# A recurrent layer gated by a feed-forward block: down projection of the gate in its own batch's stage, activation loads as ordinary steps, first gate and up weights fetched in the attention stage

## The chip, the cores and the metric

The kernel runs on one core of a Trainium2 chip. The metric is the time of one execution on the device in microseconds; the table below has three runs and one further execution, which was profiled. In the profile PE is TensorE (PEld its weight loads), DVE is VectorE, ACT is ScalarE, POOL is GpSimd, and SP is SyncE, whose queue issues nearly all DMAs here.

## The reference

Eight batches of 512 tokens with 512 features, all in float32. What is computed for each batch:

```python
xn = layernorm(x)
# recurrent part s
x_ssm, z = split(xn @ W_in.T)                    # 1024 + 1024 features
x_conv   = silu(causal_conv4(x_ssm) + conv_b)
p        = x_conv @ W_x.T                        # 16 B, 16 C, 1 step size
dt       = softplus(p[..., -1] + mean(dt_bias))
h_t      = exp(A * dt_t) * h_(t-1) + dt_t * B_t * x_t    # 1024 x 16 states
y_t      = sum_n(h_t * C_t)
s        = ((y + D * x_conv) * silu(z)) @ out_W.T
# gate g
attn = causal attention of rmsnorm(xn), 16 heads of 32; only attn @ A (rank 16) is used
mod  = 0.1 * tanh(attn @ A)
h    = rmsnorm(xn) * ln2_w
gate = silu(h @ W_in_base.T + mod * (h @ A) @ B)
up   = h @ W_up_base.T                           # 2048 features
g    = silu(xn + (gate * up) @ W_down.T)
out  = x + s * g
```

## The kernel before

The work has two stages. The first, the attention stage, runs over all eight batches: layer norm, attention down to the rank-16 modulation, and the transposed activations. It leaves for each batch `scr_x[b]` in DRAM (normalised x in its first half, the weighted `h` in the second) and the modulation in `scr_m[b]`. At its end it also does the convolutions and step sizes of batch 0 (`convolution(d)`, `steps_of_time`), and fetches xn and h of batch 0. Its tile pools are then given back, and the pools of the second stage (`wst`, `mp`, `scan`, `tmp`) are opened in their place; `wp` and `act` live through both.

The second stage is the scan. Each batch has 64 steps. A step k scans two channels of each of 32 groups for 16 states at once: a 128 x 1024 tile `x`, loaded from `scr_c` by broadcast (`load_scan`, issued four steps ahead into a ring of ten tiles), multiplied by dt*B (`inputs`, L487 on VectorE for even k, L489 on GpSimd for odd k, two steps ahead), scanned (`scan_step`, L495, VectorE, the decays written by ScalarE just before into a single `decay` buffer, L475), multiplied by C (`outputs`, L502, GpSimd). Every four steps the sum over states is a burst of small matmuls on TensorE (`sum_states`, L514), two steps after the last of the four; two bursts complete one block of 128 channels, and `finish_y` gates it with z on VectorE. The ring of `x` is released by these bursts.

Around the scan the dense work of TensorE is dealt out as a list of parts, `batch_parts(b)`. A part is a triple: its weight in units (a unit is one 128 x 128 by 128 x 512 float32 matmul), the loads it needs, and a function that issues its instructions and returns later pieces, each with a delay in chunks. A step has two chunks; in each chunk parts are issued until their units catch up with the share of the batch that has passed. The order on every engine is thus written out by the program, and each engine executes its own queue in that order. The parts of batch b, before:

- for b > 0, four times `finish(b-1, m)`: the down projection of the batch before (four parts of 4 units, L326; then `residual`, an add on VectorE and a tanh on ScalarE), the out projection (4 + 5 units, L342), then `product` (two VectorE operations, the first completes silu, the second multiplies by the out projection, L352 and L353), `turn` (four transposes), `add` (residual x) and `store`. The residual x is loaded as `fx` in `product`. The tiles are `f` and `xt`, two buffers each
- behind m = 1 an item `("h", load_h(b))`, and behind the four an item `("xn", load_xn(b+1))`
- eight pairs `gate_up` (17 units each, L275 and L284), with the convolutions of the next batch (`conv_in`, 4 units, L187) between them, and near the end `step_size(b+1)` (four projections of 2 units, then `turn`, which stores `scr_p` and reads it back three times as the broadcast B, C and dt)
- between them, eight z gates (`z_gate`, 4 units, L187, tanh L261, VectorE L255), at shares 0, 8/64, 16/64 and so on of the batch

For batches 1 to 6 this makes 136 + 32 + 64 + 36 + 9 + 32 = 309 units in 128 chunks. After the last batch the four `finish(7, m)` follow alone.

Loads go through `prefetch()`, called before and behind each part: it walks up to eight parts ahead and issues their loads in order, at most `limits[kind] - 1` outstanding of a kind, and stops at the first that it may not issue. An item of kind "xn" or "h" is issued only when it is itself the next part to run:

```python
if kind == "xn" or kind == "h":
    if state["load"] > state["run"]:
        return
```

The parts of a batch are put in the queue when its first step begins; those of batch 0 after the pools of the second stage are opened. `wgu` (gate and up weights, 512 KB, three buffers) is in the pool `wst`.

Of the kernel before, what the change touches and what calls it, by code (L numbers as in the profile page):

```python
# [10 lines left out]
F32 = mybir.dt.float32  # L11
AF = mybir.ActivationFunctionType
ALU = mybir.AluOpType
# [4 lines left out]
P = 128  # L18
NB = 8
S = 512  # L20
DM = 512
KT = DM // P
TT = S // P
DI = 1024
ND = DI // P
# [4 lines left out]
NF = 2048 // P  # L30
# [9 lines left out]
def mamba_gated_ffn_kernel(  # L40
# [22 lines left out]
    nc = tc.nc  # L63
# [18 lines left out]
    wp = ctx.enter_context(tc.tile_pool(name="w", bufs=1))  # L82
# [19 lines left out]
    def load_xn(b):  # L102
        xnt[b] = act.tile([P, KT, S], F32, tag="xnt", name=f"xnt_{b}")
        nc.sync.dma_start(xnt[b], scr_x[b][:, :KT, :])

    def load_h(b):
        ht[b] = act.tile([P, KT, S], F32, tag="ht", name=f"ht_{b}", bufs=1)
        nc.sync.dma_start(ht[b], scr_x[b][:, KT:, :])
        modh[b] = act.tile([2 * QD, S], F32, tag="modh", name=f"modh_{b}", bufs=1)
        for i in range(2):  # L110
            nc.sync.dma_start(modh[b][i * QD : i * QD + R, :], scr_m[b])
# [88 lines left out]
        loaded["win", b, c] = w  # L200

    def load_gu(b, f):
        w = wst.tile([P, 2, KT, P], F32, tag="wgu", name=f"wgu_{b}_{f}", bufs=3)
        nc.sync.dma_start(w, w_ffn[f][:, :2])
        loaded["wgu", b, f] = w

    def load_down(b, m, q):
        w = wst.tile([P, NF // 4, P], F32, tag="wd", name=f"wd_{b}_{m}_{q}", bufs=4)
        nc.sync.dma_start(w, w_ffn[ts(q, NF // 4), :, 2, m, :].rearrange("f p c -> p f c"))
        loaded["wd", b, m, q] = w  # L210
# [38 lines left out]
    def z_gate(b, d):  # L249

        st = {}

        def gate():
            t = tmp.tile([P, S], F32, tag="z", name=f"z_{b}_{d}")
            nc.vector.scalar_tensor_tensor(t, st["th"], 1.0, st["ps"], ALU.add, ALU.mult)  # L255
            gates[b, d] = t

        def run():
            ps = in_proj(b, ND + d)
            th = tmp.tile([P, S], F32, tag="th", name=f"zth_{b}_{d}", bufs=3)  # L260
            nc.scalar.activation(th, ps, AF.Tanh, scale=0.5)  # L261
            st.update(ps=ps, th=th)
            return [(1, gate)]

        return [(4, [("win", lambda: load_win(b, ND + d))], run)]
# [47 lines left out]
            (4, [], lambda: second(1)),  # L313
        ]

    def finish(b, m):

        st = {}

        def down(q):  # L320
            if q == 0:
                st["acc"] = bank(f"ps_acc_{b}_{m}")
            w = loaded.pop(("wd", b, m, q))
            for j in range(NF // 4):
                f = q * (NF // 4) + j
                nc.tensor.matmul(  # L326
                    st["acc"], lhsT=w[:, j, :], rhs=mlp[b, f], start=(f == 0), stop=(f == NF - 1)
                )
            return [(1, residual)] if q == 3 else []

        def residual():
            f = tmp.tile([P, S], F32, tag="f", name=f"f_{b}_{m}")
            nc.vector.tensor_tensor(f, st["acc"], xnt[b][:, m, :], ALU.add)
            nc.scalar.activation(st["acc"], f, AF.Tanh, scale=0.5)
            st["f"] = f

        def out_proj(q):
            if q == 0:
                st["ps"] = bank(f"ps_out_{b}_{m}")
            w = loaded["wout", b, m]  # L340
            for d in range(4 * q, 4 * q + 4):
                nc.tensor.matmul(  # L342
                    st["ps"], lhsT=w[:, d, :], rhs=xc[b, d], start=(d == 0), stop=(d == ND - 1)
                )
            if q == 1:
                loaded.pop(("wout", b, m))
                return [(1, product), (3, turn), (5, add), (7, store)]
            return []

        def product():  # L350
            f = st["f"]
            nc.vector.scalar_tensor_tensor(f, st["acc"], 1.0, f, ALU.add, ALU.mult)  # L352
            nc.vector.scalar_tensor_tensor(f, f, 0.5, st["ps"], ALU.mult, ALU.mult)  # L353
            xt = tmp.tile([P, TT, P], F32, tag="xt", name=f"fx_{b}_{m}")
            nc.sync.dma_start(xt, x[b, :, ts(m, P)].rearrange("(t p) c -> p t c", p=P))
            st["xt"] = xt

        def turn():
            ps = bank(f"ps_turn_{b}_{m}")
            for tt in range(TT):  # L360
                nc.tensor.transpose(ps[:, ts(tt, P)], st["f"][:, ts(tt, P)], ident)
            st["pt"] = ps

        def add():
            xt = st["xt"]
            nc.vector.tensor_tensor(
                xt, st["pt"].rearrange("p (t c) -> p t c", t=TT), xt, ALU.add
            )

        def store():  # L370
            nc.sync.dma_start(out[b, :, ts(m, P)].rearrange("(t p) c -> p t c", p=P), st["xt"])

        return [
            (4, [("wd", lambda q=q: load_down(b, m, q))], lambda q=q: down(q)) for q in range(4)
        ] + [
            (4, [("wout", lambda: load_out(b, m))], lambda: out_proj(0)),
            (5, [], lambda: out_proj(1)),
        ]
# [69 lines left out]
    STEPS = ND * 8  # L448
# [79 lines left out]

    def batch_parts(b):

        first = []
        if b > 0:
            for m in range(KT):
                first += finish(b - 1, m)
                if m == 1:
                    first.append((0, [("h", lambda: load_h(b))], lambda: []))
        pairs = [gate_up(b, fp) for fp in range(NF // 2)]
        convs, sizes = [], ([], [])
        if b + 1 < NB:
            convs = [conv_in(b + 1, d) for d in range(ND)]  # L540
            sizes = step_size(b + 1)
        rest = list(pairs[0])
        if b + 1 < NB:
            rest.insert(0, (0, [("xn", lambda: load_xn(b + 1))], lambda: []))
        for i in range(1, NF // 2):
            for _ in range(2 if i in (2, 4, 5) else 1):
                if convs:
                    rest += convs.pop(0)
            rest += pairs[i]
            if b + 1 < NB and i == NF // 2 - 3:  # L550
                rest += sizes[0]
            if b + 1 < NB and i == NF // 2 - 2:
                rest += sizes[1]
        parts = first + rest
        total = sum(p[0] for p in parts) + 4 * ND
        done, out_, z = 0, [], 0
        for p in parts:
            while z < ND and done >= total * (8 * z) / STEPS:
                out_ += z_gate(b, z)
                done += 4  # L560
                z += 1
            out_.append(p)
            done += p[0]
        while z < ND:
            out_ += z_gate(b, z)
            z += 1
        return out_

    queue = []
    limits = {"win": 3, "wgu": 3, "wd": 4, "wout": 2, "xn": 1, "h": 1}  # L570
    held = {}
    state = {"load": 0, "run": 0, "chunk": 0}
    later = {}

    def prefetch():
        while state["load"] < min(len(queue), state["run"] + 8):
            for kind, fn in queue[state["load"]][1]:
                if kind == "xn" or kind == "h":
                    if state["load"] > state["run"]:
                        return  # L580
                elif sum(held.values()) >= 0 and held.get(kind, 0) >= limits[kind] - 1:
                    return
                held[kind] = held.get(kind, 0) + 1
                fn()
            state["load"] += 1
# [22 lines left out]
    with ExitStack() as c1:  # L608
# [46 lines left out]
        for i in range(2):  # L655
            z = wa.tile([P, TT, HG, 4, 2 * R], F32, tag=f"z{i}", name=f"z{i}")
# [290 lines left out]
        sizes = step_size(0)  # L947

        def convolution(d):

            pair = ps_s.tile([P, 2, 512], F32, tag="s", name=f"s_conv_{d}")
            banks["special"] = lambda name: pair[:, 0, :]
            for delay, f in piece(conv_in(0, d)[0][2]):
                after(delay, f)
            banks["special"] = None
            if d + 3 < ND:
                load_win(0, d + 3)
            elif d == ND - 3:
                load_h(0)

        def steps_of_time(i):
            if i == 0:
# [83 lines left out]
    wst = ctx.enter_context(tc.tile_pool(name="wst", bufs=2))  # L1046
    mp = ctx.enter_context(tc.tile_pool(name="mp", bufs=NF))
    scan = ctx.enter_context(tc.tile_pool(name="scan", bufs=10))
    tmp = ctx.enter_context(tc.tile_pool(name="tmp", bufs=2))
# [6 lines left out]

    dtb_ps = ps_a.tile([P, S], F32, tag="dtb_ps", name="dtb_ps")

    queue.extend(batch_parts(0))
    for k in range(4):  # L1060
        load_scan(k)
        if k == 1:
            prefetch()
    inputs(0)
    inputs(1)
    decays(0)
# [1 line left out]
    for b in range(NB):  # L1068
# [3 lines left out]
        total = sum(p[0] for p in queue[n0:])  # L1072
        done = 0
        for s in range(STEPS):
            k = b * STEPS + s
# [15 lines left out]
    while bursts:  # L1091
        k = min(bursts)
# [72 lines left out]
```

## Time and profile before

| what | value |
|---|---|
| time, median of 3 runs | 3465.83 us (3461.27 to 3469.89) |
| profiled execution: its own time | 3461.55 us |
| profiled execution: span from first to last instruction | 3459.8 us, mean granted TensorE clock 0.973 |
| first scan / last scan begins | 884.80 us / 3361.76 us |
| VectorE scans, L495 | 512, mean 2285 ns |
| down projection, L326 | 1024 rows, 451.6 us busy |
| out projection, L342 | 512 rows, 226.9 us busy |
| gate and up, L275 | 2048 rows, 939.9 us busy |
| x loads for the scan | 512 of 512 KB |
| `wgu` / `win` / `wd` / `wout` loads | 128 of 512 KB / 128 of 256 KB / 128 of 256 KB / 32 of 512 KB |
| DMA over the span | 511.61 MB, 148 GB/s |

Each float32 matmul with 512 columns stands as two rows of about 0.43 us each, so a down projection of one m (16 matmuls) is 32 rows. The ends of matmuls are modelled and busy times of TensorE are unions of overlapping rows. A wait is put down to the engine or DMA that released it last.

### The profile page before, as it was taken

How to read it: one execution, taken by the hardware profiler on the slowest of the kernel's cores; microseconds unless marked ns; L12 is line 12 of the kernel's file. 1: busy time of each engine (PE TensorE's matmuls, PEld its weight loads, DVE VectorE, ACT ScalarE, POOL GpSimd, SP SyncE). 2: the span in 40 equal slices, each digit the busy share in tenths (PEclk: the TensorE clock that was granted, in tenths of full speed). 3: DMA queues.
4: the chain of work that ended last, by engine and by line, in shares of the span. 5: the costliest groups of instructions: out<-in, count | busy, mean ns of one | idle time of the engine just before them, and what ended most of it. 6: DMA issues, size and time to landing. Idle time of an engine off the chain costs nothing.

```text
span 3459.8 us, 33779 instructions
## 1 busy us (share of the span) xinstructions
PE 3224.3 (93%) x12058; PEld 1440.5 (42%) x12058; DVE 2539.9 (73%) x2782; ACT 1364.8 (39%) x2295; POOL 1898.1 (55%) x860
## 2 busy tenths in 40 slices
PE   7888888888788899999999999999999999999999
PEld 4444444444223343434344334434343444344334
DVE  5666666665688778877887887788778878878871
ACT  3555555553333333433333333334333433433330
POOL 2111111000577776677676766766776777668870
PEclk9999999998899999999999999999999999999999
DMA  3011111011766785688669666856886696779652
GB/s 111 36 41 41 41 41 41 4 50 50 190 178 166 165 222 165 170 206 219 182 156 210 188 187 162 225 170 171 197 214 178 165 215 187 187 167 231 176 136 79
DMA packets 280248, 511.61 MB, mean 148 GB/s; under 512 B 28520, under 2 KB 160104, under 8 KB 275472
## 3 DMA queue, kind: packets, MB, share of 16 engines
q1 hardware_dynamic: 278928, 501.07, 55.2%
q0 software_dynamic: 1152, 8.39, 0.6%
q8 instruction: 95, 1.56, 0.2%
q14 instruction: 73, 0.60, 0.1%
HBM read 466.55 MB, written 42.83 MB: 147 GB/s over the span
## 4 chain that ended last, share of the span: by engine, by line
PE 58%; DVE 19%; ACT 7%; POOL 7%; DMA 5%; issue 4%; SPq 1%; POOLq 0%; DVEq 0%; ACTq 0%
PE ps_acc L326 12%; PE ps_gu L275 11%; DVE x L495 8%; PE ps_in L187 6%; PE ps_out L342 6%; POOL x L502 5%; PE y L514 5%; PE ps_q L800 3%; PE ps_k L800 3%; DVE conv L226 3%; ACT decay L475 3%; PE ps_pt L846 3%; DMA win<-in_w_in 2%; PE s L815 2%; DMA x<-scr_c 2%
## 5 line engine op out<-in xcount | busy, mean ns | idle before, releaser
L502 POOL TENSOR_TENSOR x<-x,cc 128x1024 f32<-128x1024 f32 x512 | 1207.0, 2357 | 688.3 <-DVE x L495 685.2
L495 DVE TENSOR_TENSOR_SCAN x<-decay,x 128x1024 f32<-128x1024 f32 x512 | 1169.8, 2285 | 190.6 <-ACT decay L475 189.1
L475 ACT ACTIVATE decay<-dt,an 128x511 f32<-128x511 f32 x1024 | 707.6, 691 | 1219.1 <-DVE x L495 1168.5
L275 PE MATMUL ps_gu<-ht,wgu 128*128 128x512 f32 x2048 | 939.9, 609 | 6.9 <-DVE m L296 5.1
L489 POOL TENSOR_TENSOR x<-x,bb 128x1024 f32<-128x1024 f32 x256 | 603.3, 2357 | 187.4 <-DMA win<-in_w_in 186.7
L275 PEld LDWEIGHTS ps_gu<-ht,wgu 128*128 128x128 f32 x2048 | 386.3, 194 | 542.1 <-issue 503.3
L187 PE MATMUL ps_in<-xnt,win 128*128 128x512 f32 x960 | 441.4, 607 | 39.5 <-DMA win<-in_w_in 39.0
L326 PE MATMUL ps_acc<-m,wd 128*128 128x512 f32 x1024 | 451.6, 595 | 0.0
L514 PE MATMUL y<-x,sel 128*32 128x512 f32 x2048 | 304.5, 614 | 65.1 <-POOL x L502 65.1
L773 POOL TENSOR_TENSOR hT<-xnT,rms 128x512 f32<-128x512 f32 x32 | 40.9, 1277 | 559.3 <-DVE xnT L764 509.2
L487 DVE TENSOR_TENSOR x<-x,dtb_ps 128x1024 f32<-128x1024 f32 x256 | 309.1, 1207 | 45.3 <-DMA x<-scr_c 42.7
L187 PEld LDWEIGHTS ps_in<-xnt,win 128*128 128x128 f32 x960 | 183.7, 194 | 282.2 <-issue 274.1
L326 PEld LDWEIGHTS ps_acc<-m,wd 128*128 128x128 f32 x1024 | 190.8, 190 | 243.5 <-issue 242.3
L831 ACT ACTIVATE p<-s,mx 128x384 f32<-128x384 f32 (+3 forms) x512 | 240.1, 531 | 39.0 <-DVE mx L825 36.7
L846 PE MATMUL ps_pt<-ident,p 128*128 128x128 f32 x1280 | 206.4, 286 | 45.9 <-DVE pt L851 12.0
L853 ACT COPY pt<-ps_pt 128x512 f32<-128x512 f32 x224 | 127.5, 594 | 268.4 <-PE ps_pt L846 268.2
L342 PE MATMUL ps_out<-xc,wout 128*128 128x512 f32 x512 | 226.9, 594 | 0.0
L825 DVE TENSOR_REDUCE mx<-s 128x2 f32<-128x256 f32 (+3 forms) x256 | 211.1, 825 | 8.8
L846 PEld LDWEIGHTS ps_pt<-ident,p 128*128 128x128 f32 x1280 | 141.7, 142 | 153.2 <-issue 43.5
L514 PEld LDWEIGHTS y<-x,sel 128*32 128x32 f32 x2048 | 60.7, 109 | 283.1 <-issue 149.4
L226 DVE SCALAR_TENSOR_TENSOR conv<-ps_in,cw,conv 128x511 f32<-128x511 f32 x168 | 125.5, 747 | 66.5 <-ACT conv L243 62.5
L821 DVE TENSOR_TENSOR s<-s,mask 128x256 f32<-128x256 f32 x256 | 109.0, 426 | 81.9 <-PE s L815 81.3
(143 smaller groups left out, 2359.4 us busy)
## 6 DMA issues: line engine op xcount, KB each, us to landing
x<-scr_c SPq DMA_DIRECT2D x512, 512.0 KB
wgu<-in_w_ffn SPq DMA_DIRECT2D x128, 512.0 KB
win<-in_w_in SPq DMA_DIRECT2D x128, 256.0 KB
wd<-in_w_ffn SPq DMA_DIRECT2D x128, 256.0 KB
scr_c<-xc SPq DMA_DIRECT2D x64, 256.0 KB
wout<-in_out_w SPq DMA_DIRECT2D x32, 512.0 KB
xt<-in_x SPq DMA_DIRECT2D x32, 256.0 KB
scr_x<-xnT SPq DMA_DIRECT2D x8, 1024.0 KB
```

Of the source, the lines that this page charges most:

```text
L187: nc.tensor.matmul(ps, lhsT=w[:, kt, :], rhs=xnt[b][:, kt, :], start=(kt == 0), stop=(kt == KT - 1))
L275: nc.tensor.matmul(ps, lhsT=w[:, which, kt, :], rhs=ht[b][:, kt, :], start=(kt == 0), stop=(which == 1 and kt == KT - 1),)
L326: nc.tensor.matmul(st["acc"], lhsT=w[:, j, :], rhs=mlp[b, f], start=(f == 0), stop=(f == NF - 1))
L342: nc.tensor.matmul(st["ps"], lhsT=w[:, d, :], rhs=xc[b, d], start=(d == 0), stop=(d == ND - 1))
L475: nc.scalar.activation(decay[:, n, 1:], spread[b][2][:, 1:], AF.Exp, scale=an[:, g // 4, g % 4 : g % 4 + 1])
L487: nc.vector.tensor_tensor(t, t, dtb_ps.unsqueeze(1).to_broadcast([P, 2, S]), ALU.mult)
L489: nc.gpsimd.tensor_tensor(t, t, spread[b][0].unsqueeze(1).to_broadcast([P, 2, S]), ALU.mult)
L495: nc.vector.tensor_tensor_scan(t, decay.rearrange("p i t -> p (i t)"), t, 0.0, ALU.mult, ALU.add)
L502: nc.gpsimd.tensor_tensor(t, t, spread[b][1].unsqueeze(1).to_broadcast([P, 2, S]), ALU.mult)
L514: nc.tensor.matmul(y[ts(j, QD), :], lhsT=sel[:, i0 + n, :], rhs=xs[k - 3 + j][:, n, :], start=(i0 + n == 0), stop=(i0 + n == 3),)
L831: nc.scalar.activation(pr[:, 2 * i + n, :], sc[i][:, n, :w], AF.Exp, bias=mx[i][:, n : n + 1])
L846: nc.tensor.transpose(ps[:, ts(h, P)], probs[b, hg, qt][:, h, ts(kt, P)], ident)
```

## The change

The down projection leaves `finish` and becomes `down_proj(b, m)`, with four parts of 4 units, `residual` and the first half of the old `product` (silu). Its four go at the end of the list of batch b itself; `finish(b-1, m)` keeps out projection, product, turn, add and store, and comes after the first `gate_up` pair of batch b. The finished `f` of a batch are kept over the boundary, in a ring of five buffers that the `fx` tiles share. `load_xn` and `load_h` become parts of 0 units that load when they run; `load_h(b+1)` goes behind the first `down_proj` of batch b, `load_xn(b+1)` directly ahead of the convolutions. The step sizes come ahead of `down_proj` 1 and 2, the z gates five steps later in each eighth, and z has one buffer. `wgu` moves to the pool `wp`, and the parts of batch 0 are queued, and prefetched, at the last convolution of the attention stage.

```diff
     def load_gu(b, f):
-        w = wst.tile([P, 2, KT, P], F32, tag="wgu", name=f"wgu_{b}_{f}", bufs=3)
+        w = wp.tile([P, 2, KT, P], F32, tag="wgu", name=f"wgu_{b}_{f}", bufs=3)
...
-            t = tmp.tile([P, S], F32, tag="z", name=f"z_{b}_{d}")
+            t = tmp.tile([P, S], F32, tag="z", name=f"z_{b}_{d}", bufs=1)
...
-    def finish(b, m):
+    silus = {}
+
+    def down_proj(b, m):
...
-            return [(1, residual)] if q == 3 else []
+            return [(1, residual), (2, product)] if q == 3 else []
 
         def residual():
-            f = tmp.tile([P, S], F32, tag="f", name=f"f_{b}_{m}")
+            f = tmp.tile([P, S], F32, tag="f", name=f"f_{b}_{m}", bufs=KT + 1)
             nc.vector.tensor_tensor(f, st["acc"], xnt[b][:, m, :], ALU.add)
             nc.scalar.activation(st["acc"], f, AF.Tanh, scale=0.5)
             st["f"] = f
+
+        def product():
+            f = st["f"]
+            nc.vector.scalar_tensor_tensor(f, st["acc"], 1.0, f, ALU.add, ALU.mult)
+            silus[b, m] = f
+
+        return [
+            (4, [("wd", lambda q=q: load_down(b, m, q))], lambda q=q: down(q)) for q in range(4)
+        ]
+
+    def finish(b, m):
...
         def product():
-            f = st["f"]
-            nc.vector.scalar_tensor_tensor(f, st["acc"], 1.0, f, ALU.add, ALU.mult)
+            f = st["f"] = silus.pop((b, m))
             nc.vector.scalar_tensor_tensor(f, f, 0.5, st["ps"], ALU.mult, ALU.mult)
-            xt = tmp.tile([P, TT, P], F32, tag="xt", name=f"fx_{b}_{m}")
+            xt = tmp.tile([P, S], F32, tag="f", name=f"fx_{b}_{m}", bufs=KT + 1)
+            xt = xt.rearrange("p (t c) -> p t c", t=TT)
...
         return [
-            (4, [("wd", lambda q=q: load_down(b, m, q))], lambda q=q: down(q)) for q in range(4)
-        ] + [
             (4, [("wout", lambda: load_out(b, m))], lambda: out_proj(0)),
...
     def batch_parts(b):
 
-        first = []
-        if b > 0:
-            for m in range(KT):
-                first += finish(b - 1, m)
-                if m == 1:
-                    first.append((0, [("h", lambda: load_h(b))], lambda: []))
         pairs = [gate_up(b, fp) for fp in range(NF // 2)]
...
-        rest = list(pairs[0])
+        parts = list(pairs[0])
...
+        if b > 0:
+            for m in range(KT):
+                parts += finish(b - 1, m)
         if b + 1 < NB:
-            rest.insert(0, (0, [("xn", lambda: load_xn(b + 1))], lambda: []))
+            parts.append((0, [], lambda: load_xn(b + 1)))
         for i in range(1, NF // 2):
-            for _ in range(2 if i in (2, 4, 5) else 1):
+            for _ in range(2 if i == 4 else 1):
                 if convs:
-                    rest += convs.pop(0)
-            rest += pairs[i]
-            if b + 1 < NB and i == NF // 2 - 3:
-                rest += sizes[0]
-            if b + 1 < NB and i == NF // 2 - 2:
-                rest += sizes[1]
-        parts = first + rest
+                    parts += convs.pop(0)
+            parts += pairs[i]
+        for m in range(KT):
+            if m == 1:
+                parts += sizes[0]
+            if m == 2:
+                parts += sizes[1]
+            parts += down_proj(b, m)
+            if m == 0 and b + 1 < NB:
+                parts.append((0, [], lambda: load_h(b + 1)))
...
-            while z < ND and done >= total * (8 * z) / STEPS:
+            while z < ND and done >= total * (8 * z + 5) / STEPS:
...
-    limits = {"win": 3, "wgu": 3, "wd": 4, "wout": 2, "xn": 1, "h": 1}
+    limits = {"win": 3, "wgu": 3, "wd": 4, "wout": 2}
...
             for kind, fn in queue[state["load"]][1]:
-                if kind == "xn" or kind == "h":
-                    if state["load"] > state["run"]:
-                        return
-                elif sum(held.values()) >= 0 and held.get(kind, 0) >= limits[kind] - 1:
+                if held.get(kind, 0) >= limits[kind] - 1:
                     return
...
             elif d == ND - 3:
                 load_h(0)
+            elif d == ND - 1:
+                queue.extend(batch_parts(0))
+                prefetch()
...
-    queue.extend(batch_parts(0))
     for k in range(4):
         load_scan(k)
-        if k == 1:
-            prefetch()
```

## The prediction

> **What bounds the kernel now.** I read first the page's busy times, then a table of windows cut where the scan of each batch begins (the first L495 of each batch; the same table for L495 alone counts 64 scans in each), then TensorE's waits inside two of these windows, and last the timeline of the end.
>
> ```profile
> PE 3224.3 (93%) x12058; PEld 1440.5 (42%) x12058; DVE 2539.9 (73%) x2782; ACT 1364.8 (39%) x2295; POOL 1898.1 (55%) x860
> ```
>
> The table of windows, its columns being the window, its length, then busy time and count of PE, PEld, DVE, ACT and POOL, the granted clock, the DMA share and GB/s:
>
> ```profile
> 866.00:884.80 18.80, 4.17 (x46) 2.17 (x45) 6.32 (x22) 6.57 (x11) 0.00 (x0) 0.73 0.44 110
> 884.80:1180.90 296.10, 251.21 (x727) 96.79 (x728) 240.57 (x195) 115.26 (x175) 223.03 (x96) 0.93 0.68 177
> 1810.10:2130.80 320.70, 311.07 (x948) 130.11 (x948) 251.14 (x212) 118.06 (x179) 223.99 (x97) 0.98 0.73 186
> 3084.80:3364.10 279.30, 270.56 (x822) 107.22 (x822) 223.87 (x167) 101.45 (x154) 222.51 (x96) 0.99 0.74 189
> 3364.10:3459.80 95.70, 88.21 (x219) 38.54 (x218) 13.02 (x19) 2.40 (x4) 2.34 (x1) 0.96 0.25 71
> ```
>
> Batches 1 to 6 last 314 to 321 us, and TensorE is busy for 306 to 311 of it (the third row is one of them): they are TensorE's. Batch 7 has less work for it and ends in 279. Batch 0 is the exception, with TensorE idle for 296.1 - 251.2 = 44.9 us. After the last scan TensorE works for 88 of 95.7 us while all others stand still. The same windows for the down projection (L326) alone; the third number is TensorE's busy time:
>
> ```profile
> 884.80:1180.90 296.10, 0.00 (x0) 0.00 (x0) 0.93 0.68 177
> 1810.10:2130.80 320.70, 56.39 (x128) 23.84 (x128) 0.98 0.73 186
> 3364.10:3459.80 95.70, 56.18 (x128) 24.00 (x128) 0.96 0.25 71
> ```
>
> Batch 0 has none; the tail has a whole one. TensorE's waits in batch 0 (first fence) and in batch 3 (second):
>
> ```profile
> engine line waited for: us in total, times, longest us
> PE y L514 <- POOL x L502: 34.1, 16, 4.9
> PE ps_in L187 <- DMA win<-in_w_in: 16.3, 2, 11.6
> PE ps_gu L275 <- DVE m L296: 2.7, 1, 2.7
> PE ps_gu L275 <- DMA wgu<-in_w_ffn: 1.8, 1, 1.8
> ```
>
> ```profile
> PE y L514 <- POOL x L502: 4.4, 4, 1.9
> PE ps_in L187 <- DMA win<-in_w_in: 4.0, 1, 4.0
> ```
>
> In batch 0 TensorE runs out of work and waits for the scan. In batch 3 its only wait for a load is the first z weight of the batch, since a batch's parts enter the queue only when it begins; no wait falls where the activations are loaded. The tail's timeline:
>
> ```profile
> 3369.98 14.00 PE L326 MATMUL ps_acc<-m,wd 128*128 128x512 f32 x32
> 3383.82 7.03 PE L342 MATMUL ps_out<-xc,wout 128*128 128x512 f32 x16
> 3390.68 7.03 PE L326 MATMUL ps_acc<-m,wd 128*128 128x512 f32 x16
> ```
>
> **The change part by part.**
>
> *Down projection of the same batch.* The instruction counts on all engines stay. Batches 1 to 6 gain one down projection and lose one: nothing on TensorE. Batch 7 gains its own for batch 6's: nothing. The tail loses 56.2 us and batch 0 gains it.
>
> The tail now: the last y matmuls end at 3370 either way (they wait for POOL after the last scan), then 4 x 6.87 us of out projection and two transposes of 0.44 us reach 3398.4; the end of the chain after the last out projection was 5.8 us (3453.97 to 3459.75). Two small terms: one of the two VectorE products has moved out (-0.7), but `fx` now shares the ring of `f`, so the last residual load waits for the transposes of m=2, which stand right behind the last out projection. Its 256 KB need at least 1.1 us at the rate below, and about 3 with issue and receipt by my estimate, against some 1.5 us of product and transposes: +2. The loads of `wout` 2 and 3 wait for the out projection two before, so they have 7 us each; alone on the queue that suffices. Tail gain: 56.2 - 2 + 0.7, taken as **-54**.
>
> Batch 0: two bounds. If its busy time simply adds, 251.2 + 56.4 = 307.6, with the 9 us of idle that other batches keep, 317: +21. But those 251.2 us are stretched: batch 3's 311.1 without down (56.4), out (226.9/8 = 28.4) and turns (about 2.4) is 224 for the same work. With down it is 280, and with batch 7's 8.7 us idle 289: -7. Here a rule enters. The row: clock 0.93 in batch 0 and 0.73 before it, 0.98 in batch 3. The Trainium skill, *TensorE: Matmul & The Clock Gate*, "The HAM clock gate", says that an idle window of about 3.4 us halves the clock until as long a busy one has passed; the waits of 4.9 us are such. With the gaps filled, the rule gives back 251 x (1 - 0.93/0.98) = 13 us of the busy time, so 304; without it 317. The trace's comparison with batch 3 gives 289. The start also gains: scan 0 starts at 884.80, scan 1 only at 895.15, against some 4.9 us a step elsewhere, because ScalarE stood 13.0 us in its queue behind the tanh of the first z gate, which waited for its weights (decays behind it, the scan behind these). With the first two gate/up weights loaded in the attention, and z gates five steps later, that is -5. What is late next: `load_xn(1)` now stands directly ahead of the first convolution, and in batch 0 SP runs little ahead, so 1 MB (4 us at the rate below, 6 with latency) is partly exposed, and ScalarE's bias pass waits in front of the decays: +5, which eats it. I take 297, nearest to batches 3 and 7: **+1**, ends -8 and +21.
>
> *Prefetch no longer blocked.* The activation loads become ordinary steps. In batches 1 to 6 no TensorE wait lies at either load, so I cost the unblocking at 0; the cover is that SP is ahead of TensorE there (about 8 us: `xnt` issued at 1596.7, the out projection before it ended at 1604.8). `load_h` (1 MB and two of 32 KB) moves to behind the first down projection of the batch before: SP issues it between `wd` loads, which have three parts (10 us) of lead, and it used to stand in the same surroundings; 0, and at most 4 us a batch if the lead is short.
>
> *Start of a batch.* The first load is now `wgu`, 512 KB instead of 256 KB. But the step-size spread (scr_p and its three reads, for which SP stood 3.8 us and then issued four x loads at once) is some 15 units of TensorE earlier, so SP comes to the boundary sooner. Between all of the 4.0 us saved and 2 us more: -1.
>
> *The out projections close together.* Four `wout` loads, four `fx` loads and four stores, formerly spread over 100 units of parts, now fall into 36 units and a z gate. A batch has 309 units in 128 chunks, so these 40 are 8.3 steps or 41 us. In that time pass 8.3 x loads (4.35 MB), three wout (1.57), fx and stores (2.1), xnt (1.05), about two wgu and three win (1.8): 10.9 MB. What the DMA engines reach with such traffic, from the window of one batch's finish, and for contrast the one behind it:
>
> ```profile
> 1500.00:1605.00 105.00, 104.22 (x320) 43.19 (x319) 76.61 (x57) 35.77 (x53) 77.50 (x34) 1.00 0.89 217
> 1605.00:1700.00 95.00, 92.60 (x276) 36.56 (x275) 78.90 (x68) 37.11 (x57) 65.11 (x29) 1.00 0.62 173
> ```
>
> 217/0.89 = 244 GB/s, so 10.9 MB take 45 us where 41 are there. The Trainium skill, *DMA: Bandwidth & Descriptors*, has pieces of 512 bytes at line rate ("Specifications") and a fit of 2.0 us + bytes/436 GB/s ("Anatomy of one DMA", for the GpSimd path): `wout`, 3.2 us, would always come in time and this part cost 0. The measured 244 decides: up to 4 us a batch. `wout` m+1 is issued when the out projection m-1 is done, 7 us before it is needed; new waits stand in SP's queue too (`fx` m for the transposes of m-1), with `wout` and x loads behind them. The scan loads have some 12 us of margin (issued 4 steps ahead, used 2.5 later), which spreads it: +2.
>
> Start and out projections together: +1 for each of seven batches, **+7**, ends -20 and +35. The z ring of one buffer costs 0: writer and last reader are both VectorE, in order. Down's products and tanh are the same ones at other places; POOL's queue is not touched.
>
> Sum: -54 + 1 + 7 = **-46**. The profiled execution took 3461.55 us, 4.3 below the median of 3465.83 of the runs shown; on the median's scale 3465.8 - 46 = **3420**.
>
> **The rivals.** (a) As above: 3420, chance 0.64.
> (b) Better: the batch starts lose their 4 us and the out projections cost nothing, 7 x -3.5 = -24, batch 0 at 289: -54 - 7 - 24 = -85, 3381. For it: SP is freed earlier at the boundary. Against: 512 KB for 256, and DMA at 0.89. Chance 0.14.
> (c) Batch 0 does not absorb: its ScalarE and VectorE queues stop behind each down tanh and it takes 317 or more: -54 + 21 + 7 = -26, 3440; were nothing absorbed, 3475. Against: batches 1 to 6 do 87 us of TensorE work more than batch 0 (56.4 + 28.4 + 2.4) in 20 us more. Chance 0.12, with 0.02 of it within 0.3%.
> (d) Slower: `wout` and `xnt` come late in every batch from 1 to 7. TensorE then waits three times 3 to 4 us for `wout` and 4 for `xnt`, some 14 us a batch, 98 in all: -54 + 1 + 98 = +45, 3511. It passes +10 us from 9 us a batch on. For it: 45 us of transfers in 41. Against: 12 us of margin on x, and before the change `xnt` and `wgu` together (1.5 MB) arrived in the 8 us that SP had. Chance 0.10: 0.06 above the bound, 0.02 within it, 0.02 still faster.
> That the change does not do what it says: the prefetch part may bring nothing at all; (a) already counts it as nothing.
>
> **How the numbers follow.** What a measurement of this kernel can tell from no change is about 0.3%, 10 us. Slower: 0.06, of (d). Within: 0.02 of (c) and 0.02 of (d), 0.04. Faster: 0.90. The likeliest sum is 3420; its unknown terms (-20 to +35, -8 to +21) rarely fall to one side together. From 3395 to 3450 leaves out most of (b) and most of (d), under 2 in 10.
>
> **What would show it.** Right: after the last scan some 42 us without any down projection; batch 0 with 128 down rows, near 297 us, clock above 0.93; batches 1 to 6 within a few us of 317. A wait of TensorE for `wout` or `xnt` by the DMA speaks for (d), no DMA wait at batch starts for (b). Wrong: middle batches over 325 us, or batch 0 over 320.

## The result, and the profile after

| | before | after |
|---|---|---|
| median of five runs each | 3464.66 us (3460.68 to 3469.89) | 3444.8 us (3433.01 to 3452.24) |
| ratio | | 0.9936, 95% interval 0.9911 to 0.9962 |
| profiled execution (span) | 3461.55 (3459.8) | 3433.01 (3431.2) |

The change makes the kernel 20 us faster in the median; 46 us were forecast. The time of 3444.8 us lies inside the forecast range of 3395 to 3450. Seven more runs of the changed kernel gave 3447.94 (ratio 0.994). The profiled execution is the fastest of its five, so its 28.6 us overstate the median's gain. Cutting both profiles at the first scan of each batch and at the start of the last scan (3361.8 before, 3388.8 after):

| stretch | before | after | difference | forecast |
|---|---|---|---|---|
| up to the first scan | 884.8 | 883.5 | -1.3 | 0 |
| batch 0 | 296.1 | 314.8 | +18.7 | +1 |
| batches 1 to 6 | 1903.9 | 1920.8 | +16.9 | +6 |
| batch 7, to its last scan | 277.0 | 269.7 | -7.3 | +1 |
| last scan to the end | 98.0 | 42.4 | -55.6 | -54 |

The tail did as forecast, and what it gave was partly taken back in batches 0 to 6. Batch 7, which loads no activations for a next batch, became shorter. The windows of batch 0, 3, 7 and the tail after, with the same columns as before (window, length, busy time and count of PE, PEld, DVE, ACT and POOL, clock, DMA share, GB/s):

```profile
883.50:1198.30 314.80, 281.06 (x842) 113.64 (x841) 244.54 (x203) 117.68 (x179) 224.49 (x97) 0.96 0.71 182
1840.50:2160.90 320.40, 307.74 (x947) 129.05 (x946) 250.65 (x213) 117.80 (x179) 224.24 (x97) 0.97 0.74 186
3119.10:3388.80 269.70, 263.90 (x803) 104.40 (x802) 220.48 (x166) 100.83 (x153) 220.69 (x95) 1.00 0.73 183
3388.80:3431.20 42.40, 34.90 (x99) 14.67 (x97) 10.22 (x13) 0.60 (x1) 3.20 (x2) 0.95 0.24 68
```

The same windows for the down projection alone, now L328:

```profile
883.50:1198.30 314.80, 58.23 (x128) 24.59 (x128) 0.96 0.71 182
1840.50:2160.90 320.40, 59.38 (x128) 25.04 (x128) 0.97 0.74 186
3388.80:3431.20 42.40, 1.02 (x3) 0.19 (x1) 0.95 0.24 68
```

Batch 0 now holds a down projection and the tail none but its last three rows. TensorE's busy time in batch 0 grew from 251 to 281 us and its idle time fell from 45 to 34, but the batch became longer. TensorE's longest waits say where, first in batch 0, then in batch 3 after (us in total, times, longest).

```profile
PE ps_in L187 <- DMA xnt<-scr_x: 13.1, 1, 13.1
PE y L527 <- POOL x L515: 10.1, 6, 5.3
PE ps_gu L275 <- DVE m L296: 5.9, 2, 4.1
```

```profile
PE ps_in L187 <- DMA xnt<-scr_x: 7.9, 1, 7.9
PE ps_gu L275 <- DMA wgu<-in_w_ffn: 1.6, 1, 1.6
```

The first lines are new: the first convolution waits for its activations. The old wait at the start of a batch (4.0 us for `win`) is down to 1.6 us for `wgu`. In the whole execution the new wait is

```profile
PE ps_in L187 <- DMA xnt<-scr_x: 60.2, 7, 13.1
```

The timeline of SP's queue and of TensorE around the one in batch 3:

```profile
1884.90 0.64 SPq L479 DMA_DIRECT2D x<-scr_c  x1
1885.59 0.62 SPq L104 DMA_DIRECT2D xnt<-scr_x  x1
```

```profile
1886.07 3.60 PE L357 MATMUL ps_out<-xc,wout 128*128 128x512 f32 x8
1897.60 5.50 PE L187 MATMUL ps_in<-xnt,win 128*128 128x512 f32 x8 [7.93 <-DMA xnt<-scr_x]
```

The load is issued at 1885.59, TensorE has finished the last out projection at 1889.67 and the load releases it at 1897.60: a lead of 4.1 us against 12.0 us from issue to use. At the old place, in the kernel before, the same kind of load was issued and first used at

```profile
1596.67 0.35 SPq L104 DMA_DIRECT2D xnt<-scr_x  x1
1625.38 3.60 PE L187 MATMUL ps_in<-xnt,win 128*128 128x512 f32 x8
```

The DMA engines of the changed kernel in the 12 us from issue to use, in two windows, and then over the whole stretch of the out projections:

```profile
1885.60:1891.00 5.40, 4.07 (x13) 1.77 (x11) 4.81 (x5) 1.38 (x2) 4.71 (x3) 1.00 1.07 268
1891.00:1897.60 6.60, 0.00 (x0) 0.00 (x0) 1.60 (x1) 1.38 (x2) 4.64 (x2) 0.76 1.04 313
1848.00:1890.00 42.00, 41.67 (x129) 17.61 (x127) 34.25 (x29) 14.08 (x22) 33.54 (x15) 1.00 0.85 215
```

In the 12 us they are full, a share of 1.07 and 1.04 (a packet counts whole in the window in which it begins, so a share can pass 1). Over the 42 us of the out projections the share is 0.85: the crowd comes at their end. The packets of 8192 bytes, which are those of xnt, begin only at 1891.3 in the trace: 5.7 us pass behind x, `fx` and stores that were issued before it. In batches 1 to 6 these packets begin 4.9 to 6.1 us after the issue and end 10.2 to 11.7 us after it. In the kernel before they began 0.6 to 1.0 us after it and ended after 4.5 to 5.0 us. So the new place took from the load both its lead and its quick landing.

The tail's timeline, against the 14.00 + 7.03 us for each m before:

```profile
3396.72 14.00 PE L357 MATMUL ps_out<-xc,wout 128*128 128x512 f32 x32
3410.55 0.60 PE L376 MATMUL ps_turn<-ident,f 128*128 128x128 f32 x4
3410.99 7.03 PE L357 MATMUL ps_out<-xc,wout 128*128 128x512 f32 x16
```

The out projections follow one another without a wait for `wout`.

### The profile page after: what moved, and what is told of

It reads as the page before. It is cut to its first block, busy times and chain, and to the rows that moved or that the text cites. A ratio compares the mean times of both kernels' runs of the same rounds, so it can differ in the third digit from the quotient of the medians.

```text
span 3431.2 us, 33790 instructions
## 1 busy us (share of the span) xinstructions
PE 3201.5 (93%) x12058; PEld 1435.9 (42%) x12058; DVE 2537.0 (74%) x2782; ACT 1363.4 (40%) x2295; POOL 1900.6 (55%) x860
## 5 line engine op out<-in xcount | busy, mean ns | idle before, releaser
L275 PE MATMUL ps_gu<-ht,wgu 128*128 128x512 f32 x2048 | 920.4, 599 | 17.3 <-DVE m L296 12.7
L187 PE MATMUL ps_in<-xnt,win 128*128 128x512 f32 x960 | 451.1, 616 | 69.7 <-DMA xnt<-scr_x 60.2
L328 PE MATMUL ps_acc<-m,wd 128*128 128x512 f32 x1024 | 469.2, 613 | 7.9 <-DMA wd<-in_w_ffn 7.9
L328 PEld LDWEIGHTS ps_acc<-m,wd 128*128 128x128 f32 x1024 | 198.3, 197 | 264.4 <-issue 248.3
L527 PE MATMUL y<-x,sel 128*32 128x512 f32 x2048 | 273.6, 603 | 14.8 <-POOL x L515 14.8
L856 PEld LDWEIGHTS ps_pt<-ident,p 128*128 128x128 f32 x1280 | 141.5, 142 | 152.9 <-issue 44.6
```

The source lines that it names most:

```text
L187: nc.tensor.matmul(ps, lhsT=w[:, kt, :], rhs=xnt[b][:, kt, :], start=(kt == 0), stop=(kt == KT - 1))
L275: nc.tensor.matmul(ps, lhsT=w[:, which, kt, :], rhs=ht[b][:, kt, :], start=(kt == 0), stop=(which == 1 and kt == KT - 1),)
L328: nc.tensor.matmul(st["acc"], lhsT=w[:, j, :], rhs=mlp[b, f], start=(f == 0), stop=(f == NF - 1))
L527: nc.tensor.matmul(y[ts(j, QD), :], lhsT=sel[:, i0 + n, :], rhs=xs[k - 3 + j][:, n, :], start=(i0 + n == 0), stop=(i0 + n == 3),)
L856: nc.tensor.transpose(ps[:, ts(h, P)], probs[b, hg, qt][:, h, ts(kt, P)], ident)
```

## The experiments

Theory A: the gains of tail and batch starts are as large as they should be, and the wait for xnt takes most of them back. Rivals: the DMA queues are over-full in the out projections, so that something waits there wherever xnt stands; batch 0 has no room for the down projection.

**The changed kernel again.** No edit.

> The changed kernel once more, beside the others on the same chip. Its five runs lay between 3433 and 3452 us, about 20 us below before. If the waits of TensorE for xnt (13 us in batch 0, some 8 us in each of batches 1 to 6) are the missing part of the forecast, this profile has them again, 55 to 65 us in all. Expected 3435 to 3450.

Median 3447.94 us (3432.53 to 3451.17), ratio 0.994 (0.9917 to 0.9963). The wait for xnt is there again, 62.1 us in seven times. The kernel before had 20 runs beside it, from 3453.4 to 3477.0.

**xnt early.** In `batch_parts`:

```diff
         parts = list(pairs[0])
+        if b + 1 < NB:
+            parts.insert(0 if b == 0 else len(parts), (0, [], lambda: load_xn(b + 1)))
...
-        if b + 1 < NB:
-            parts.append((0, [], lambda: load_xn(b + 1)))
```

> load_xn(b+1) stands ahead of the four out projections instead of behind them (in batch 0 ahead of the first gate_up pair). Theory A, the wait for xnt is what the forecast lacked: TensorE no longer waits at the first convolution, about 13 us in batch 0 and 8 us in each of six batches go, 61 us at most; 3385 to 3400. Theory B, the DMA queues are full in the out projections: with 1 MB ahead of them wout comes late, TensorE waits for it as long as it did for xnt, and the time stays within 15 us of the changed kernel, 3430 or more.

Median 3381.71 us (3375.7 to 3387.55), ratio 0.9756 (0.9731 to 0.9781): 66 us under the changed kernel and 85 under the kernel before, both run beside it. Batch 0 is 310 us, batches 1 to 6 are 310 to 312. The wait is gone and none for `wout` has come; TensorE's waits in batch 3:

```profile
PE ps_acc L328 <- DMA wd<-in_w_ffn: 2.0, 1, 2.0
PE ps_in L187 <- DVE m L296: 1.8, 1, 1.8
PE ps_gu L275 <- DVE m L296: 1.5, 1, 1.5
```

Theory A holds, and the rival of over-full queues falls for the kernel as a whole: the same bytes pass, in another order, without holding up TensorE. A second time this version gave 3388.94, ratio 0.9782 (0.9759 to 0.9806):

> The version with the early xn load once more, beside the one that leaves out work in batch 0 on the same chip. Four runs lay between 3376 and 3388 us; expected 3376 to 3390, and batch 0 at 310 us, batches 1 to 6 at 310 to 312 without a wait of TensorE for xnt.

The time lies at the upper end of the expectation; batches 4 to 6 were 313 to 315 us in its profile.

**xnt early in batch 0 alone.** The same edit under `b == 0`.

> Only the xn load of batch 0 is moved ahead, the others stay behind the out projections. Theory A: only the wait of batch 0 goes, 13 us of TensorE and with it ScalarE's wait ahead of the decays; batch 0 falls from 315 to about 300 us, total 10 to 15 us below the changed kernel. Rival: batch 0 is at TensorE's own limit with the down projection in it, and gives back less than 5 us.

3438.56 us (3432.08 to 3445.2), 9 us under the changed kernel; the intervals of the two ratios (0.9898 to 0.9942 against 0.9917 to 0.9963) overlap. In the profiles batch 0 falls from 315 and 317 to 310 us, by about half of the 13 us that TensorE waited. By the ratios some 57 us of the early load (48 by its second result) are then left for batches 1 to 6, 8 to 9.5 us for each. That is the wait, and the slow matmuls behind it: the eight rows at 1897.60 above took 5.50 us, and with the early load eight such rows take

```profile
1866.54 3.60 PE L187 MATMUL ps_in<-xnt,win 128*128 128x512 f32 x8
```

The six waits of the changed kernel (6.7 to 9.2 us) sum to 47 us, the slow rows behind them (5.2 to 6.7 us for each eight) add 12: 59 us, where batches 1 to 6 are 58 us shorter in the first profile of the early load (1862.7 us) and 49 in the second (1871.8).

**Unblocking alone, in the kernel before.**

```diff
-                    first.append((0, [("h", lambda: load_h(b))], lambda: []))
+                    first.append((0, [], lambda: load_h(b)))
...
-            rest.insert(0, (0, [("xn", lambda: load_xn(b + 1))], lambda: []))
+            rest.insert(0, (0, [], lambda: load_xn(b + 1)))
```

> The kernel before with one part of the change alone: its loads of xn and h become ordinary steps, at their old places, so that the weights behind them are prefetched past them. As predicted, no TensorE wait lay at these loads, so it costs and brings nothing: within 5 us of before. Rival: the blocked prefetch did cost something that the waits do not show, and it is 10 us or more faster.

3465.73 against 3466.44 us, ratio 0.9999 (0.9985 to 1.0013). This part of the change, alone, shows no effect. What cost time was the new place of the xn load, not its form.

**xnt late, its use later.** The changed kernel, with the number of convolutions ahead of pairs 1 to 7 changed:

```diff
-            for _ in range(2 if i == 4 else 1):
+            for _ in range((0, 2, 1, 2, 1, 1, 1)[i - 1]):
```

> The changed kernel with load_xn at its new place behind the out projections, but the first convolution one gate_up pair later (two convolutions behind pair 1 in place of one ahead of it), 17 units or some 17 us of TensorE work more between load and use. Theory A, the load had too short a lead: the waits for xnt go as when the load is moved ahead, 3380 to 3395. Theory B, the DMA queues of the out projections are over-full, and moving the megabyte ahead of them was what helped: the load still comes behind the crowd, wgu of pair 1 now waits behind it, and at least half of the 66 us between the changed kernel and the one with the early load stays away, 3412 or more.

3408.31 us (3405.5 to 3411.91), ratio 0.9841 (0.9822 to 0.9859): between what the two theories expected, nearer to B's 3412. TensorE's waits in batch 3:

```profile
PE ps_gu L275 <- DVE m L296: 3.8, 1, 3.8
PE ps_gu L275 <- DMA wgu<-in_w_ffn: 3.1, 1, 3.1
```

No wait for xnt is left, so 17 units of lead are enough. The order brings two waits of its own: one for VectorE where the early load has 1.5 us, and 3.1 us for `wgu`, as Theory B had it in kind but not in size. Over batches 1 to 6 the wait for `wgu` comes twice (3.5 us together), the one for VectorE six times (23.0 us against 8.7 with the early load). Of the 36 us by which these batches are longer than with the early load, TensorE is idle for 17.5 and busy for 18.5 at the same work. So it is mainly the order that costs time here, and not the DMA queues.

**xnt in quarters.** `load_xn` at its new place, as four loads:

```diff
-        nc.sync.dma_start(xnt[b], scr_x[b][:, :KT, :])
+        for kt in range(KT):
+            nc.sync.dma_start(xnt[b][:, kt, :], scr_x[b][:, kt, :])
```

> The changed kernel with load_xn at its new place, but as four loads of 256 KB, one for each of the four matmul steps of the convolution's projection, so that the first matmul waits for a quarter. In the changed kernel xnt is issued about 4 us before TensorE wants it and lands 12 us after issue. Theory A1, half of these 12 us is the queue of loads issued ahead of it (x, fx and stores): the wait for the first quarter stays at 3 to 5 us of the 8, the time falls by 20 to 35 us, to 3410 to 3425. Theory A2, the megabyte itself is what takes the time: the first quarter is there in time, nearly the whole 59 us of batches 1 to 6 go, 3390 or less.

3427.53 us (3423.43 to 3443.21), ratio 0.9886 (0.9864 to 0.9907), some 18 us under the changed kernel by the ratios, just short of what A1 expected. The wait in batch 3:

```profile
PE ps_in L188 <- DMA xnt<-scr_x: 6.0, 1, 6.0
```

In all seven batches it is 44.7 us where the changed kernel has 60.2. So the larger part of the wait is the queue ahead of the load, the smaller the megabyte itself. A2 falls.

**The first weights not fetched in the attention.** The early load, with `queue.extend(batch_parts(0))` and its `prefetch()` back where they stood before.

> The version with the early xn load, with the first gate and up weights no longer fetched in the attention: the parts of batch 0 are queued where they were before the change. Theory: TensorE waits for them at the start of the scan, and ScalarE's tanh stands behind it with the decays, so 5 to 12 us are lost in the first steps of batch 0; 3387 to 3394. Rival: the first scan steps have room and batch 0 is set by TensorE later, below 4 us.

3387.94 us, ratio 0.978 (0.976 to 0.9801), 6 us above the early load's first result and 1 under its second: the times show no difference. The profile does: the first eight steps of batch 0 last 44.6 us against 39.0, the whole batch 313 us against 310, and TensorE's first `ps_gu` has an idle stretch of 12.1 us before it. By the profile this part of the change is worth some 3 to 6 us.

**Step sizes late.** The early load, with `sizes[0]` at `m == 2` and `sizes[1]` at `m == 3`.

> The version with the early xn load, with the step sizes 16 units later (projections ahead of down projection 2, transposes, store and the three reads ahead of 3), 16 units from the end of the batch as before the change. Theory: SP then stands for the scr_p round trip close to the boundary again, the first weights of each batch come late and TensorE waits 3 to 4 us at each of seven batch starts; 20 to 28 us more, 3402 to 3410. Rival: the wait at the batch starts went because gate and up, not the z gate, come first there, or because SP is no longer held by wd waits; then it stays away, within 6 us of 3382.

3418.56 us (3415.22 to 3422.66), ratio 0.987 (0.9851 to 0.9889), 37 us above the early load's first result and 30 above its second, more than the 20 to 28 expected. In the whole execution TensorE has

```profile
PE ps_gu L275 <- DMA wgu<-in_w_ffn: 40.0, 7, 6.2
```

where the early load has 1.1 us in two times. The step sizes' earlier place is what removed the wait at the batch starts. With them late, batches 1 to 6 take 1903.7 us and batch 7 277.9, as in the kernel before (1903.9 and 277.0): what these batches gain without the wait for xnt, they owe to this place. The wait it removed is 6 us here rather than the 4 us of before; that the first load is now `wgu` with twice the bytes may be why, and no run tests it.

**Batch 0 without most of its down projection.** The early load, leaving out 14 of 16 matmuls of each down projection of batch 0:

```diff
                 f = q * (NF // 4) + j
+                if b == 0 and 0 < f < NF - 1:
+                    continue
```

> The version with the early xn load, leaving out 14 of the 16 matmuls of each down projection in batch 0 alone (its result for that batch is cut to two terms); parts, units and the order of all else stay. What is left of batch 0's growth then is order and pace, not TensorE's work. Batch 0 is 310 us there and was 296 before. Theory A, TensorE's work is the growth: batch 0 falls to 290 to 298, total 12 to 20 us lower, 3362 to 3370. Theory B, the waits of ScalarE and VectorE behind each part, or the pace of the parts, set it: under 5 us.

3386.75 us (3375.41 to 3389.48), no gain. Batch 0 lasts 310.2 us, as with its matmuls. The last part of batch 0, first of the early load, then without the matmuls:

```profile
1121.00:1198.40 77.40, 75.37 (x260) 34.72 (x259) 57.44 (x51) 29.45 (x45) 56.96 (x26) 0.96 0.84 205
```

```profile
1117.00:1194.60 77.60, 45.81 (x141) 17.58 (x142) 55.49 (x49) 28.93 (x44) 56.33 (x26) 0.70 0.77 169
```

TensorE has 30 us less to do there, and the stretch is no shorter. The waits of TensorE that came in place of the matmuls (9.0 us for `wgu`, 4.3 for `wd`) did not lengthen it either. So the down projection's matmuls are hidden, as forecast, and yet batch 0 grew from 296 to 310 us. The trace says where: the first down projection of batch 0 starts in step 42 (at 1102.3 in the changed kernel). The 24 steps from step 40 on take 108.4 us there and took 107.8 before, while the first 40 steps, with no down projection in them, grew from 188.3 to 206.4 us.

**The same, with the pace of before.** In addition batch 0's down parts count 1 unit and its step sizes come one down projection earlier (not in the lines shown), so that the other parts are spread over nearly the whole batch: 225 units in 128 chunks, where it was 209 before the change and 273 with it. A version with 0 units gave no result.

```diff
-            (4, [("wd", lambda q=q: load_down(b, m, q))], lambda q=q: down(q)) for q in range(4)
+            (4 if b else 1, [("wd", lambda q=q: load_down(b, m, q))], lambda q=q: down(q)) for q in range(4)
...
```

> As the kernel that leaves out 14 of the 16 matmuls of each down projection in batch 0 (its result for that batch is cut to two terms); in addition batch 0's down parts count 1 unit instead of 4, and its step sizes stand one down projection earlier, so that the other parts are dealt out over nearly the whole batch again (225 units in 128 chunks; 209 before the change, 273 with it). Leaving the matmuls out alone left batch 0 at 310 us. Theory A, the pace is batch 0's growth: gate, up and convolution come closer together and fill TensorE in steps 8 to 40; batch 0 falls to 288 to 298. Theory B, the VectorE and ScalarE work and the loads of the down projection, which stay, are the growth: batch 0 stays at 305 or more.

3399.0 us; batch 0 lasts 318 us. By its number that is Theory B (305 or more), and A's 288 to 298 did not come. But the batch divides. Its first 40 scan steps, in the kernel before, with the early load, and here:

```profile
884.80:1073.10 188.30, 160.95 (x445) 58.54 (x445) 151.94 (x120) 71.36 (x108) 141.82 (x61) 0.95 0.71 191
```

```profile
888.40:1087.70 199.30, 178.70 (x503) 68.34 (x504) 160.41 (x134) 75.61 (x115) 141.36 (x61) 0.95 0.71 185
```

```profile
892.60:1080.30 187.70, 161.12 (x434) 58.12 (x434) 151.48 (x120) 72.02 (x109) 139.11 (x60) 0.93 0.66 175
```

At the slower pace they take 187.7 us, as before the change; at the faster one 199.3, with 18 us more work on TensorE and 9 more on VectorE in the same steps. The down projection's VectorE and ScalarE work, which B blames, lies behind these steps. The 24 steps left take 130.0 us here against 110.7 with the early load; waits of TensorE for `wd`, 17.7 us in three times, are this experiment's own, so the whole of batch 0 can't be read from it. For the first 40 steps it is shown that the pace makes the 11.6 us. That a slower pace would give them back to the whole batch is not shown, and the other 2 to 3 us of the 14 are open.

**A candidate for the best.** The early load, and the order of the kernel with the later convolutions in batch 0 alone.

> A candidate for the best version: the early xn load, and in batch 0 alone the first convolution behind pair 1 and two behind it, as in the kernel with the later convolutions, where batch 0 took 304 us against 310. If the order of batch 0's parts sets its length, as leaving out its down projection left it unchanged, the time is 4 to 7 us under the version with the early load, 3375 to 3378. If the early load had already taken what there is, within 2 us of 3382.

3380.66 us (3368.31 to 3385.49), ratio 0.9733 (0.9711 to 0.9756). Batch 0 is 306.5 us against 310. The interval overlaps that of the early load's first result (0.9731 to 0.9781) and just misses that of its second (0.9759 to 0.9806): no clear difference is shown. Both beat the two kernels of this study by 1.5% and more.

## Why the prediction was right or wrong

- *The tail, -54.* Right: -55.6, and no wait for `wout` in it. Nor does VectorE wait there for the last residual load, for which 2 us were taken off.
- *Unblocking the prefetch, 0.* Right: ratio 0.9999 alone.
- *The new place of xnt, 0 in batches 1 to 6.* This is the step that failed. "The cover is that SP is ahead of TensorE there (about 8 us ...)" took SP's lead from the old place, where xnt was issued 8 us ahead of the end of the out projections, landed within 5 us and was used only at 1625.4, 29 us after its issue. At the new place the lead is 4.1 us: between 1850 and 1886 SP stands 12.5 us for the buffers of `wout`, 8.2 for stores and 5.1 for the bursts of y. And the load needs 12.0 us, twice the 6 that I gave it in batch 0. Cost: 8 us of wait in each of six batches, 8 to 10 us of time. Rival (d) had xnt as the smaller part of its price (4 us, beside 9 to 12 for `wout`). The sizes were the other way round: xnt 8, `wout` 0.
- *The out projections close together, +2 a batch.* The estimate of 45 us of transfers in 41 was too high: over 42 us of them the DMA share is 0.85. Only the end is over-full (1.07 and 1.04), and "up to 4 us" missed whom that would hit: not `wout`, but the load last in line with no lead. The rule of the Trainium skill that I set aside, *DMA: Bandwidth & Descriptors*, "Anatomy of one DMA" (2.0 us + bytes/436 GB/s, for the GpSimd path), gives an estimate of 4.4 us for the megabyte. At the old place its last packet ended 4.5 to 5.0 us after the issue; at the new one 12.0 us were measured to its use, 5.7 of them before its first packet. With the rule the term would have been smaller still.
- *The start of a batch, -1.* Right in its reason, too small. Before, the seven waits for the first z weight sum to 27.5 us, and the slow matmuls behind five of them (5.25 to 5.37 us for eight rows) add 9; I counted 4.0 us a batch and set 512 KB against it. Without the wait for xnt batches 1 to 6 are 32 to 41 us shorter than before and batch 7 is 5; with the step sizes put back late, 30 to 37 us return. SP's earlier arrival outweighs the doubled load.
- *Batch 0, +1.* 297 became 315. TensorE's busy time came as the comparison with batch 3 had it, 281 us against 280 (the rule on the clock made it 295). The idle time was taken from batch 7, 8.7 us, and was 33.7. The exposed xnt load was priced at 5 us and is worth 5 to 7 of time with a wait of 13.1. The rest, 14 us, is no work of the down projection. I left out that 273 units instead of 209 in 128 chunks bring gate, up and convolution 30% closer together in the first 40 steps, while the 24 steps behind them, which hold the down projection, hardly grow (107.8 to 108.4 us). The pace is a term that the sum lacked. The start, -5, is borne out by the profile alone (44.6 to 39.0 in the first eight steps).
- *Rival (c)* had nearly these numbers, batch 0 at 317 and 3440 in all, but by another cause: queues that stop behind each down tanh. The growth lies ahead of the first down projection.
- *The clock.* 0.96 in batch 0 after 0.93, in the direction of the rule; the 13 us that I worked out from it can't be seen in the batch's length.
- *The bound.* I took 0.3% as what a measurement can tell. Twenty runs of the kernel before spread by 0.7%.

That the time lies inside the range, and that neither sign of being wrong came (batch 0 over 320, middle batches over 325), is luck: in batches 1 to 6 a wait of 49 to 58 us and a gain of 32 to 41, both taken as next to nothing, cancel to +17. With the early load the profiles differ from the kernel before by +4 us up to the first scan, +14 in batch 0, -41 in batches 1 to 6, -5 in batch 7 and -57 behind the last scan, -86 in all; the medians by -85, in its second result by -78. Rival (b)'s 3381 is the early load's time, but not its sum: (b) had batch 0 at -7 and the other batches at -24.

## What to carry to other kernels

When a load is moved in a program's order, its lead must be read at the new place: how far the issuing queue is ahead of the user there, what is in the DMA queues ahead of it, and how long after its issue it lands. A lead or a landing time measured at the old place says nothing of the new one, nor does the absence of a wait there. When parts are dealt out in proportion, adding parts at the end also brings all the earlier ones closer together.

## What the runs showed of the hardware

- 1 MB loaded into a full queue took 12.0 us from issue to use, of which 5.7 us passed before its first packet; at the old place, in the kernel before, its last packet ended within 5.0 us of the issue. Splitting it in four shortened the wait in batch 3 only from 7.9 to 6.0 us.
- A wait of TensorE cost more than its length. Behind the waits for xnt of 6.7 to 9.2 us eight matmul rows took 5.2 to 6.7 us, where they take 3.60 without a wait. At the batch starts of the kernel before, eight rows took 3.67 us behind waits of 2.8 and 3.75 us, and 5.25 to 5.37 behind the five others (3.5 to 4.7 us).
- Leaving out 30 us of TensorE's work in a stretch of 77 us let the granted clock fall from 0.96 to 0.70; the stretch kept its length. Work taken off TensorE there gave nothing back.
- The start of the first scan alone lay between 883.5 and 893.1 us in the profiles, in a stage that these versions hardly touch. This is part of the spread between runs.
